# A third layer every sixteenth step: the units of a small network folded once more by DMA

## The chip, the cores and the metric

The kernel runs on one core of one Trainium2 chip. The metric is the time of one execution on the device, in microseconds (us). The kernel before was run three times; one more execution was profiled.

## What is computed

The reference chains four layers on an image of 2 x 512 channels x 32 x 32 pixels. Only the first, a deformable attention block, is touched here. Of it, one piece matters: a bias on the attention scores that a small network of three layers computes for each pair of a pixel and a sampling point.

```
pos  = grid_q[:, :, None, :] - grid_kv[:, None, :, :]
bias = jnp.sign(pos) * jnp.log1p(jnp.abs(pos))
bias = jax.nn.relu(bias @ cpb_w1 + cpb_b1)
bias = jax.nn.relu(bias @ cpb_w2 + cpb_b2)
bias = (bias @ cpb_w3 + cpb_b3).reshape(b, GROUPS, H * W, Hd * Wd)
sim  = jnp.einsum('bhid,bhjd->bhij', qh, kh) + bias
attn = jax.nn.softmax(sim, axis=-1)
```

There are 2 images with 8 groups of 64 points each, 1024 pixels, and 128 hidden units in both hidden layers. The second layer (128 to 128 units, for 1024 points x 1024 pixels) is by far the largest piece of work of the whole kernel.

## The kernel before

**Tiling.** A unit of the work is a period `t` (NT = 8 of them): 128 points, two groups. It is cut into NR = 32 steps, and a step has four points; the loop over `i` (L813) runs over all 256 steps. For each point `first` (L515) makes the first layer on VectorE in one custom instruction: 128 units on the partitions, 1024 pixels along the row, the sum of an x table and a y table, cut off below at zero. Its result stands in a ring of eleven tiles (L182 to L184); the points run AHEAD = 7 ahead of the step that uses them (L808).

**Second layer.** `second` (L536) multiplies on TensorE. The 128 output units are cut into four parts of 32 (BLOCK), taken in the order 1, 0, 3, 2. For one part, the four points of the step stand beside one another: each product takes 32 columns of the array and writes 32 partitions of a PSUM tile `z`, so a tile is four points x 32 units on the partitions and 1024 pixels along the row. There are three such PSUM tiles. ScalarE applies the bias and the relu (L552) into an SBUF tile `h2`. The weights of the third layer were taken into the second one beforehand as magnitudes; only their signs (`turn`, `w3sign`) are left to be applied.

**Folding the units.** Since the third layer only sums over units, with signs, units can be added before it. `joined` (L555) adds parts 0 and 1 on VectorE, and parts 2 and 3; then a DMA on POOL that accumulates (L832, 512 KB) adds the second sum to the first. What is left is one tile a step, four points x 32 units. Two steps then share a tile. For an even step a DMA on POOL adds the odd partitions to the even ones (L825, 256 KB), so that 16 units for each point stand on the even partitions. SP copies the even partitions of the odd step's tile to the odd partitions of the even step's (L827), and a DMA on POOL adds the odd step's odd partitions to that (L829).

**Third layer.** At every eighth step (`due`, L837) `third` (L562) multiplies four such tiles, eight points each, by a matrix of signs `w3`, into the score tile `sim` of the period. Four products stand beside one another, 32 columns each, for each half of the pixels. A slice of `w3` that begins at 24 - r puts the eight columns that aren't zero at the right rows. After the last one of a period `scores` (L575) adds the products of queries and keys, and a new chain of small pieces of work starts: `finish` of this period (softmax, transposes), `offsets` of the period after the next, `samples` of the next one. The loop takes one piece of that chain after the second and the fourth part of a step (L834, `next(behind, None)`). The last four steps of all go another way, in `finish_last` (L641).

**Order.** Nothing is scheduled by a planner: `in_order` (L60) holds each engine to the order in which the program issues its instructions, POOL's and SP's DMAs among them. What a queue waits for holds all that stands behind it.

**Tables.** `load_tabs` (L496) fetches the x and y tables for sixteen points (four steps) at a time, from DRAM, spread to all partitions: two quarters of eight points each. ScalarE scales them (L513). A quarter of the period's points is what one of the four column groups of `third` gets.

**Buffers.** The part-0 tiles, which live on as the joined ones, come from `h2p` (6 tiles, even steps) and `h2j` (3 tiles, odd steps), parts 2 from `h2b` (3), parts 1 and 3 from `h2q` (3). `simb` and `at` of the softmax come from a pool of two.

Of the kernel before, what the change touches and what calls it, by code (L numbers as in the profile page):

```python
# [19 lines left out]
P = 128  # L20
# [12 lines left out]
RCH = 8  # L33
# [47 lines left out]
def kernel(ctx: ExitStack, tc: tile.TileContext, a: dict, out: bass.AP):  # L81
# [56 lines left out]
    def layer0(l0, fold_d, t2_b, o2_b):  # L138
# [6 lines left out]
        h2j = l0.enter_context(tc.tile_pool(name="att_h2j", bufs=3))  # L145
# [79 lines left out]
        for w in (w3, w3_4):  # L225
            nc.gpsimd.memset(w, 0.0)
# [5 lines left out]
        def bias_weights():  # L232
# [3 lines left out]
            few = one.tile([P, 26], F32, name="few")  # L236
# [68 lines left out]
            nc.vector.tensor_scalar(w3[:, 24:32], w3[:, 24:32], w3sign[:, 1:2], None, ALU.mult)  # L305
            magnitude(b2h, w3_of)
# [186 lines left out]
        NCH = 2 * NR // RCH  # L493
        tabs_of = {}

        def load_tabs(c):  # L496

            t, rc = divmod(c, NCH)
            assert t in tables
            tabs_of[c] = []  # L500
            for ax in range(2):
                src = slog_d[t, ax].rearrange("(q r) i -> q r i", q=4)
                tab = two.tile([P, 2, RCH, 32], F32, name=f"tab{ax}")
                q, r = rc % 2 * 2, rc // 2 * RCH
                nc.sync.dma_start(out=tab, in_=src[q : q + 2, r : r + RCH, :].partition_broadcast(P))
                tabs_of[c].append(tab)
# [8 lines left out]
        def first(p):  # L515

            chunk, quad = divmod(p, 2 * RCH)
            quad, point = divmod(quad, RCH)
            if quad == 0 and point == 0:
                tabs_of.pop(chunk - 1, None)  # L520
                if chunk + 1 < NT * NCH:
                    load_tabs(chunk + 1)
            tx, ty = tabs_of[chunk]
            h1 = ring[p % len(ring)]

            nc.vector._custom_dve(  # L526
                TENSOR_ADD_SAT,
                out=h1.rearrange("p (y x) -> p y x", x=W),
                in0=tx[:, quad, point, :].unsqueeze(1).to_broadcast([P, H, W]),
                in1=ty[:, quad, point, :].unsqueeze(2).to_broadcast([P, H, W]),  # L530
                s0=float(np.finfo(np.float32).max),
                s1=0.0,
            )
            return h1

        def second(i, h1s, part):  # L536
# [13 lines left out]
            ring = h2q if part % 2 else h2b if part else h2j if i % 2 else h2p  # L550
# [11 lines left out]
        def third(sim, r, h2s, fours=(), halves=range(2)):  # L562

            for half in halves:
                n = slice(half * HALF, (half + 1) * HALF)
                ways = [(quad, w3[:, 24 - r : 56 - r], h2) for quad, h2 in enumerate(h2s)]
# [16 lines left out]
        def finish(t, sim):  # L583
# [4 lines left out]
            simb = two.tile([P, HW], F32, name="simb", tag="simb")  # L588
# [10 lines left out]
            at = two.tile([P, 8, P], F32, name="at", tag="simb")  # L599
# [41 lines left out]
        def finish_last(sim, eights, fours):  # L641
# [6 lines left out]
            simb = two.tile([P, HW], F32, name="simb", tag="simb")  # L648
# [7 lines left out]
            at = two.tile([P, 8, P], F32, name="at", tag="simb")  # L656
# [156 lines left out]
        for i in range(steps):  # L813
            for k, part in enumerate((1, 0, 3, 2)):
# [8 lines left out]
                if i < steps - 2:  # L823
                    if i >= 2 and i % 2 == 0 and k == 0:
                        nc.gpsimd.dma_start(out=joins[i - 2][0:P:2], in_=joins[i - 2][1:P:2], accum_op=ALU.add)  # L825
                    if i >= 3 and i % 2 and k == 0:
                        nc.sync.dma_start(out=joins[i - 3][1:P:2], in_=joins[i - 2][0:P:2])  # L827
                    if i >= 3 and i % 2 and k == 3:
                        nc.gpsimd.dma_start(out=joins[i - 3][1:P:2], in_=joins.pop(i - 2)[1:P:2], accum_op=ALU.add)  # L829
                if k == 1 and i - 1 in parts:  # L830
                    other = joined(parts.pop(i - 1), 2)
                    nc.gpsimd.dma_start(out=joins[i - 1], in_=other, accum_op=ALU.add)  # L832
                if k % 2:
# [4 lines left out]
                if k == 1 and due >= 0 and due % 8 == 0:  # L838
# [3 lines left out]
                    third(sim, r, [joins.pop(due + j) for j in range(0, 8, 2)])  # L842
                    if r == NR - 8:
# [1336 lines left out]
```

## Time and profile before

| | us |
|---|---|
| median of 3 runs (lowest, highest) | 3402.58 (3399.19, 3405.2) |
| the profiled execution's own time | 3400.25 |
| its span in the profile | 3398.4 |
| from the first to the last product of the second layer | 57.2 to 2001.4 |

| in that stretch of 1944.2 us | busy us |
|---|---|
| TensorE (products) | 1932.5 |
| VectorE | 1852.0 |
| ScalarE | 1412.1 |
| GpSimd (POOL) | 440.6 |
| the 16 DMA engines, mean share | 0.67 |

The profile gives for each group of equal instructions the line of the program, the engine, what is written and read, the count, then the busy time in all and the mean of one in ns, then the idle time of the engine just before them and what ended most of it. Busy time of the products is a model: they are pipelined and overlap, four of them at once where they take 32 columns each, so the time that a piece of work takes on TensorE is read better from the distance of one start to the next. A row of the timeline has the start, the time that it took, engine, line and operation, how many alike were merged into it, and in brackets the idle time before it and what ended that.

### The profile page before, as it was taken

The numbers are of one execution on the slowest core, as the hardware profiler recorded it, in microseconds if no ns is written. First come the engines' busy times: TensorE is split into PE (matmuls) and PEld (weight loads), VectorE is DVE, ScalarE is ACT, GpSimd is POOL, SyncE is SP. The second block draws the span as 40 slices with busy tenths as digits, with TensorE's granted clock in tenths as the row PEclk, the third lists the DMA queues.
The fourth block names the chain that finished last, engine by engine and source line by source line (L and its number), as shares of the span: only waits on it lengthen the run. The fifth ranks groups of instructions, "written<-read, shape, count | busy, mean of one in ns | idle before, by whom it ended". The sixth has DMA issues, their size and how long they took to land.

```text
span 3398.4 us, 61331 instructions
## 1 busy us (share of the span) xinstructions
PE 3351.9 (99%) x24853; PEld 1615.5 (48%) x24853; DVE 2662.6 (78%) x3461; ACT 1803.4 (53%) x2764; POOL 464.0 (14%) x563
## 2 busy tenths in 40 slices
PE   9999999999999999999999999999999999999998
PEld 4333332333333333333333338999953533678676
DVE  6999999999997899999998954455456465756565
ACT  4866867867866667867867641112136245212221
POOL 0222222222221122222222210000000000000000
PEclk9999999999999999999999999999999999999999
DMA  5676676676775576676776641000100010000110
GB/s 167 149 151 139 141 153 143 139 153 138 148 149 118 110 150 138 149 148 137 150 147 142 141 124 57 14 11 11 51 0 14 26 35 14 7 7 5 28 38 30
DMA packets 146707, 320.31 MB, mean 94 GB/s; under 512 B 31088, under 2 KB 76784, under 8 KB 145648
## 3 DMA queue, kind: packets, MB, share of 16 engines
q0 software_dynamic: 56880, 199.79, 30.9%
q1 hardware_dynamic: 88240, 111.80, 10.9%
q8 instruction: 198, 3.24, 0.4%
q10 hardware_dynamic: 1296, 4.72, 0.4%
q14 instruction: 93, 0.76, 0.1%
HBM read 71.46 MB, written 10.83 MB: 24 GB/s over the span
## 4 chain that ended last, share of the span: by engine, by line
PE 77%; DVE 16%; issue 4%; ACT 2%; DMA 1%; ACTq 0%; POOL 0%; DVEq 0%; SPq 0%; POOLq 0%
PE z L543 35%; DVE wa L526 6%; PE pma L136 5%; PE pw L1392 5%; PE pmb L136 4%; DVE h L557 4%; PE pmv L1392 4%; PE score L1568 3%; PE pv L1580 3%; PE pm L1392 3%; PE score L1392 3%; DVE h L526 2%; PE pmp L136 2%; PE pp L629 2%; PE ppr L1392 1%
## 5 line engine op out<-in xcount | busy, mean ns | idle before, releaser
L543 PE MATMUL z<-wa,cpb_w 128*32 128x512 f32 x11904 | 1779.1, 593 | 6.7 <-DVE simbias L490 3.4
L552 ACT ACTIVATE h<-z,b2h 128x1024 f32<-128x1024 f32 x1024 | 1134.2, 1114 | 529.6 <-PE z L543 506.2
L543 PE MATMUL z<-h,cpb_w 128*32 128x512 f32 x4480 | 986.3, 593 | 3.3 <-ACT h L552 2.2
L543 PEld LDWEIGHTS z<-wa,cpb_w 128*32 128x32 f32 x11904 | 492.9, 110 | 883.6 <-issue 804.6
L526 DVE CUSTOM_DVE_ANT_1 wa<-tab,tab 128x1024 f32<-128x1024 f32 x744 | 878.2, 1216 | 34.0 <-PE z L543 33.9
L557 DVE SCALAR_TENSOR_TENSOR h<-h,turn,h 128x1024 f32<-128x1024 f32 x512 | 653.3, 1276 | 8.8 <-ACT h L552 8.6
L543 PEld LDWEIGHTS z<-h,cpb_w 128*32 128x32 f32 x4480 | 256.2, 110 | 335.0 <-issue 291.8
L832 POOL DMA_DIRECT2D h<-h x255 | 227.9, 894 | 1055.0 <-DVE h L557 711.4
L526 DVE CUSTOM_DVE_ANT_1 h<-tab,tab 128x1024 f32<-128x1024 f32 x280 | 332.9, 1216 | 10.5 <-PE z L543 10.4
L1214 ACT COPY p<-pma 128x128 f32<-128x128 f32 x70 | 18.6, 266 | 305.6 <-PE pma L136 305.6
L1569 ACT ACTIVATE p<-score 128x512 f32<-128x512 f32 x256 | 130.0, 626 | 81.2 <-PE score L1568 80.4
L1206 DVE TENSOR_TENSOR upper<-pma,p 128x256 f32<-128x256 f32 x70 | 29.5, 421 | 163.6 <-ACT p L1214 163.5
L825 POOL DMA_DIRECT2D h<-h x126 | 110.9, 880 | 322.4 <-DMA h<-h 319.0
L829 POOL DMA_DIRECT2D h<-h x126 | 119.0, 944 | 155.2 <-DMA h<-h 148.8
L1601 DVE TENSOR_TENSOR acc<-acc,p 128x1024 f32<-128x1024 f32 x96 | 111.1, 1217 | 20.7 <-ACT p L1569 20.6
L1568 PE MATMUL score<-q,k 64*128 64x512 f32 x512 | 120.7, 604 | 1.1 <-DVE gm L1088 1.1
L1580 PE MATMUL pv<-p,vT 128*64 128x512 f32 x512 | 116.5, 598 | 0.0
L1392 PE MATMUL pw<-p,vT 128*128 128x256 f32 x384 | 91.5, 385 | 6.9 <-DVE p L1853 6.9
L513 ACT ACTIVATE tab<-tab,pc 128x512 f32<-128x512 f32 x126 | 96.2, 763 | 0.0
L1392 PE MATMUL pmv<-wa,hc 128*128 128x256 f32 x384 | 89.7, 380 | 5.2 <-DVE u L1413 5.2
L347 ACT ACTIVATE products<-qpad,pc 128x64 f32<-128x64 f32 x252 | 85.5, 407 | 0.0
L1392 PEld LDWEIGHTS pw<-p,vT 128*128 128x128 f32 x384 | 72.4, 191 | 24.2 <-DVE p L1853 8.4
(432 smaller groups left out, 3680.2 us busy)
## 6 DMA issues: line engine op xcount, KB each, us to landing
h<-h POOLq DMA_DIRECT2D x255, 512.0 KB, 5.0
h<-h POOLq DMA_DIRECT2D x252, 256.0 KB, 4.7
tab<-slog_d SPq DMA_DIRECT2D x128, 256.0 KB, 4.6
h<-h SPq DMA_DIRECT2D x126, 256.0 KB, 2.3
r<-d SPq DMA_DIRECT2D x24, 256.0 KB, 3.5
xt<-in_xt SPq DMA_DIRECT2D x8, 512.0 KB, 7.6
wa<-in_mlp_w SPq DMA_DIRECT2D x4, 1024.0 KB, 7.9
wb<-in_mlp_w SPq DMA_DIRECT2D x16, 256.0 KB, 5.6
```

What stands on the lines that cost most here:

```text
L136: nc.tensor.matmul(pm, w, m, start=(k == 0), stop=(k == len(pairs) - 1))
L526: nc.vector._custom_dve(TENSOR_ADD_SAT, out=h1.rearrange("p (y x) -> p y x", x=W), in0=tx[:, quad, point, :].unsqueeze(1).to_broadcast([P, ...
L543: nc.tensor.matmul(z[point * 32 : point * 32 + 32, n], cpb_w2[:, lo : lo + 32], h1s[point][:, n], start=True, stop=True,)
L552: nc.scalar.activation(h2, z, AF.Relu, bias=b2h[:, part : part + 1])
L557: nc.vector.scalar_tensor_tensor(h2, h2, turn[:, part // 2 : part // 2 + 1], parts.pop(part + 1), ALU.mult, ALU.add)
L829: nc.gpsimd.dma_start(out=joins[i - 3][1:P:2], in_=joins.pop(i - 2)[1:P:2], accum_op=ALU.add)
L832: nc.gpsimd.dma_start(out=joins[i - 1], in_=other, accum_op=ALU.add)
L1392: nc.tensor.matmul(out, stationary(l, k), moving(r, k), start=start and k == 0, stop=k == nk - 1, skip_group_check=not start,)
L1568: nc.tensor.matmul(sc, ks[m][r, s * P : (s + 1) * P], qs[m][r, n], start=True, stop=True)
L1569: nc.scalar.activation(p[:, part], sc, AF.Exp, scale=64 ** -0.5)
L1580: nc.tensor.matmul(pv[half][part * 64 : part * 64 + 64], vt[s % 4][:, lo : lo + 64], lps[s, half][:, part, :], start=(s == 0), stop=(s == 7),)
L1601: nc.vector.tensor_add(acc[half], acc[half], ps[s, half])
```

## The change

It folds the units once more for the first 240 steps (all but the last sixteen). `LAST` is 240.

- Each step's tile is folded from 32 units to 16 (256 KB) in a DMA of its own on POOL, issued at the first part of the step after the next. A step whose number divides by four then folds its own tile to 8 units (128 KB). The other three steps of four copy 32 partitions into that tile (128 KB, SP), and one more accumulating DMA (128 KB, POOL) adds their other 32 partitions there. So four steps share a tile, sixteen points x 8 units.
- The third layer comes every sixteenth step, with four tiles of sixteen points and a matrix `w3_16`. It is issued after the fourth part of step due + 19, where due is the first step of its sixteen; before, it was issued after the second part of step due + 11. The chain of small pieces of a period thus starts half a step later.
- Points are taken quarter by quarter: a table holds sixteen points of one quarter in one run, where it held eight of two quarters. For the last sixteen steps the old order is kept, with the old scheme of folding.
- `h2p` now holds the tiles of every fourth step, `h2j` (now 4 tiles) the others. `simb` and `at` come from a pool of one and so share one buffer; `at` of `finish_last` comes from `h2q`.
- The weights' preparation gets four small VectorE operations for the new column pattern and two for the matrix.

```diff
-        h2j = l0.enter_context(tc.tile_pool(name="att_h2j", bufs=3))
+        h2j = l0.enter_context(tc.tile_pool(name="att_h2j", bufs=4))
...
+            quarter = few[:, 26:28]
+            for k in range(2):
+                nc.vector.tensor_reduce(quarter[:, k : k + 1], ident[:, 2 + k : P : 4], AX.X, ALU.add)
+                nc.vector.scalar_tensor_tensor(eighth, quarter[:, k : k + 1], 8.0, eighth, ALU.mult, ALU.add)
+            nc.vector.tensor_scalar(w3_16[:, 16:32], row[:, 0:16], eighth, 0.0, ALU.add, ALU.is_equal)
+            nc.vector.tensor_scalar(w3_16[:, 16:32], w3_16[:, 16:32], w3sign[:, 1:2], None, ALU.mult)
...
-        NCH = 2 * NR // RCH
+        NCH = NR // 4
+        LAST = NT * NR - 16
...
-                tab = two.tile([P, 2, RCH, 32], F32, name=f"tab{ax}")
-                q, r = rc % 2 * 2, rc // 2 * RCH
-                nc.sync.dma_start(out=tab, in_=src[q : q + 2, r : r + RCH, :].partition_broadcast(P))
+                tab = two.tile([P, 16, 32], F32, name=f"tab{ax}")
+                if 4 * c < LAST:
+                    q, r = rc % 4, rc // 4 * 16
+                    nc.sync.dma_start(out=tab, in_=src[q, r : r + 16, :].partition_broadcast(P))
+                else:
+                    q, r = rc % 2 * 2, 16 + (rc - 4) // 2 * 8
...
-            ring = h2q if part % 2 else h2b if part else h2j if i % 2 else h2p
+            ring = h2q if part % 2 else h2b if part else h2j if i % (4 if i < LAST else 2) else h2p
...
-        def third(sim, r, h2s, fours=(), halves=range(2)):
+        def third(sim, r, h2s, fours=(), halves=range(2), wide=False):
...
-                ways = [(quad, w3[:, 24 - r : 56 - r], h2) for quad, h2 in enumerate(h2s)]
+                w = w3_16[:, 16 - r : 48 - r] if wide else w3[:, 24 - r : 56 - r]
+                ways = [(quad, w, h2) for quad, h2 in enumerate(h2s)]
...
-            simb = two.tile([P, HW], F32, name="simb", tag="simb")
+            simb = one.tile([P, HW], F32, name="simb", tag="simb")
...
-            at = two.tile([P, 8, P], F32, name="at", tag="simb")
+            at = one.tile([P, 8, P], F32, name="at", tag="simb")
...
-                if i < steps - 2:
-                    if i >= 2 and i % 2 == 0 and k == 0:
+                if LAST <= i - 2 and i < steps - 2:
+                    if i % 2 == 0 and k == 0:
                         nc.gpsimd.dma_start(out=joins[i - 2][0:P:2], in_=joins[i - 2][1:P:2], accum_op=ALU.add)
...
+                if 0 <= i - 2 < LAST:
+                    j = (i - 2) % 4
+                    whole, own = joins[i - 2 - j], joins[i - 2]
+                    if k == 0:
+                        nc.gpsimd.dma_start(out=own[0:P:2], in_=own[1:P:2], accum_op=ALU.add)
+                    if k == 3 and j == 0:
+                        nc.gpsimd.dma_start(out=own[0:P:4], in_=own[2:P:4], accum_op=ALU.add)
+                    if k == 3 and j:
+                        nc.sync.dma_start(out=whole[j:P:4], in_=own[0:P:4])
                 if k == 1 and i - 1 in parts:
                     other = joined(parts.pop(i - 1), 2)
                     nc.gpsimd.dma_start(out=joins[i - 1], in_=other, accum_op=ALU.add)
+                j = (i - 3) % 4
+                if k == 1 and 0 <= i - 3 < LAST and j:
+                    nc.gpsimd.dma_start(
+                        out=joins[i - 3 - j][j:P:4], in_=joins.pop(i - 3)[2:P:4], accum_op=ALU.add
+                    )
...
                 due = i - 11
-                if k == 1 and due >= 0 and due % 8 == 0:
+                if k == 1 and due == LAST:
+                    third(sim, 16, [joins.pop(due + j) for j in range(0, 8, 2)])
+                due = i - 19
+                if k == 3 and 0 <= due < LAST and due % 16 == 0:
                     t, r = divmod(due, NR)
                     if r == 0:
                         sim = ps_s.tile([P, HW], F32, name="sim")
-                    third(sim, r, [joins.pop(due + j) for j in range(0, 8, 2)])
-                    if r == NR - 8:
+                    third(sim, r, [joins.pop(due + j) for j in range(0, 16, 4)], wide=True)
+                    if r:
```

## The prediction

> **What bounds the kernel now.** I read the page first: the busy shares, the costliest groups, the DMA issues.
>
> ```profile
> PE 3351.9 (99%) x24853; PEld 1615.5 (48%) x24853; DVE 2662.6 (78%) x3461; ACT 1803.4 (53%) x2764; POOL 464.0 (14%) x563
> ...
> L543 PE MATMUL z<-wa,cpb_w 128*32 128x512 f32 x11904 | 1779.1, 593 | 6.7 <-DVE simbias L490 3.4
> ...
> L543 PE MATMUL z<-h,cpb_w 128*32 128x512 f32 x4480 | 986.3, 593 | 3.3 <-ACT h L552 2.2
> ...
> L526 DVE CUSTOM_DVE_ANT_1 wa<-tab,tab 128x1024 f32<-128x1024 f32 x744 | 878.2, 1216 | 34.0 <-PE z L543 33.9
> ...
> h<-h POOLq DMA_DIRECT2D x255, 512.0 KB, 5.0
> h<-h POOLq DMA_DIRECT2D x252, 256.0 KB, 4.7
> ...
> h<-h SPq DMA_DIRECT2D x126, 256.0 KB, 2.3
> ```
>
> The second layer's products (L543) run from 57.2 to 2001.4 us, and in all that time TensorE idles 10 us in front of them (6.7 + 3.3). VectorE's first layer (L526) waits for TensorE. So TensorE bounds this stage, and an instruction taken off it is worth its own length, if VectorE follows. The windows of three periods (32 steps each) tell how closely it must follow:
>
> ```profile
> 564.50:804.80 240.30, 239.07 (x2176) 74.52 (x2172) 232.96 (x213) 179.38 (x251) 55.82 (x65) 1.00 0.68 145
> 804.80:1045.10 240.30, 239.07 (x2176) 74.51 (x2172) 232.97 (x213) 179.39 (x251) 55.87 (x65) 1.00 0.70 144
> 1045.10:1315.90 270.80, 268.29 (x2240) 85.59 (x2236) 237.98 (x217) 179.85 (x251) 55.89 (x65) 1.00 0.60 129
> ```
>
> After the time stand PE, PEld, DVE, ACT, POOL, the clock, the DMA share. A period takes 240.3 us and VectorE works 233.0 of them: 7.3 us to spare. The granted clock is full. The third period holds four output projections and is longer for that.
>
> Then the timeline of TensorE at one third layer, and that of VectorE before and after it:
>
> ```profile
> 859.67 0.60 PE L543 MATMUL z<-h,cpb_w 128*32 128x512 f32 x3
> 860.10 1.90 PE L571 MATMUL sim<-h,w 128*32 128x512 f32 x16
> 861.81 0.59 PE L543 MATMUL z<-wa,cpb_w 128*32 128x512 f32 x1
> ```
>
> ```profile
> 841.91 2.35 DVE L526 CUSTOM_DVE_ANT_1 wa<-tab,tab 128x1024 f32<-128x1024 f32 x2
> 844.18 1.28 DVE L557 SCALAR_TENSOR_TENSOR h<-h,turn,h 128x1024 f32<-128x1024 f32 x1
> 845.38 2.35 DVE L526 CUSTOM_DVE_ANT_1 h<-tab,tab 128x1024 f32<-128x1024 f32 x2
> ...
> 850.00 1.23 DVE L526 CUSTOM_DVE_ANT_1 h<-tab,tab 128x1024 f32<-128x1024 f32 x1 [0.95 <-PE z L543]
> ```
>
> Groups of four products start every 0.43 us (859.24, 859.67, 860.10). A step is 16 groups, 6.86 us; a third layer is four groups, 860.10 to 861.81: **1.71 us**. VectorE repeats two firsts and a join every 3.47 us (841.91 to 845.38), so a step costs it 6.94 us, more than TensorE's bare 6.86. It catches up only while TensorE does something else.
>
> Last, POOL's queue, its whole traffic over two steps:
>
> ```profile
> 846.00 0.86 POOL L832 DMA_DIRECT2D h<-h  x1 [5.12 <-DMA h<-h]
> 846.54 1.19 POOL L829 DMA_DIRECT2D h<-h  x1
> 851.05 0.84 POOL L825 DMA_DIRECT2D h<-h  x1 [3.33 <-DMA h<-h]
> 853.85 0.86 POOL L832 DMA_DIRECT2D h<-h  x1 [1.95 <-DVE h L557]
> ```
>
> Behind each 512 KB sum (L832) the next fold stands in the queue until that sum has landed: 846.00 to 851.05.
>
> **What the skill says.** The Trainium skill, "TensorEngine Tiling (Array Packing)", Available Configurations: a 128x32 setting gives four independent tiles. The trace agrees: four products of 593 ns every 0.43 us. "DMA: Bandwidth & Descriptors", Issuing engines are not separate DMA queues: what SP and POOL issue shares the same 16 engines, so the new folds add to the load of the sums. The trace's one DMA share (0.68 to 0.70) is of these 16. Same page, Rules for kernel authors: an accumulating DMA must wait for the semaphore of an earlier one on the same bytes. The waits "<-DMA h<-h" above are that. "SBUF — State Buffer", SBUF: two separate sides: DMA traffic and engine accesses don't slow one another. The trace fits: VectorE's join took 1262 to 1286 ns through all 507 accumulating DMAs of POOL. So more DMAs should not lengthen VectorE's work.
>
> **The change, part by part.**
>
> *Third layers.* Before, 31 stand in the loop (L571, 496 products there, 16 each) and one in the finish. After, seven periods have two each; the last has a wide one and, in the old scheme, one at step 251: 16. So 15 x 1.71 = **25.7 us** leave TensorE. None lay under other work, since TensorE is the bound. The wide ones have the same shape (four tiles, 32 columns).
>
> *VectorE as the next limit.* Over a period TensorE will need 240.3 - 2 x 1.71 = 236.9 us, VectorE still 233.0. In 16 bare steps TensorE takes 16 x 6.86 + 1.71 = 111.5 us, VectorE 16 x 6.94 = 111.0. So on the mean it follows. Locally it is tight. From 850.00 to 944.55 VectorE has no gap, because the offsets' reductions (L353, six of about 0.9 us) come on top. I followed the margin, from the end of the last first that a step needs to that step's first product: 5.0 us at step 11 of the period, 1.5 us at steps 18 and 19 (step 18's last first is done at 905.0, its products begin at 906.5), 5.7 at step 22. The third layer at 860.10 lies inside this stretch and goes; 1.5 - 1.7 = -0.2, so TensorE will wait some 0.2 to 0.6 us at step 18. In the periods that start at 57.2 and 1045.1 the margin falls to 0.3 already, but there the stretch begins early or behind the projections and doesn't lose 1.7 in the same way. I take 0.4 us x 5 periods = 2 us; bounds 0 and 12 (1.7 in seven periods).
>
> *The folds on POOL and the DMA engines.* Before, two steps need two sums of 512 KB, two accumulating folds of 256 KB and one copy of 256 KB. After, each of the first 240 steps has its sum and its own 256 KB fold (same count), and a new 128 KB accumulate; three steps of four have a 128 KB copy on SP. So 240 more issues on POOL: 240 x 0.84 = 202 us of a queue that is busy 56 of 240 us, hidden. Engine time: POOL's queue takes 30.9% of 16 engines for 199.79 MB, or 84 engine-us per MB, so 128 KB cost 11.0 / 16 = 0.69 us of all engines; 240 of them 166 us. The copies move 25 MB in place of 33, about -26 us. That is +140 of 1944 us: the share rises from 0.67 to about 0.74. A 32-row accumulate isn't in the trace: the 256 KB one lands after 3.2 at best, less half its data time (0.69) 2.5 us alone; behind a 512 KB sum about 5. From above the median 4.7 of the larger DMA, from below the estimate of 2.3 us by the DMA page (Anatomy of one DMA: 2.0 us and the bytes by 436e3), which for 512 KB gives 3.2 where the trace has at least 4.5. I take 5.3 behind a sum.
>
> *Who waits.* In order on POOL: sum, last accumulate, own fold, each fourth step the second fold. A second fold that waits (own fold of the same step, about 5 us) holds the next own fold and the next sum, which can't start before anyhow. On SP a copy that waits for its fold holds a table load (needed three steps, 20 us, later). The qpad memset (L324, 1.5 us) moves half a step and stands behind two accumulates; ACT needs it half a step, 3.5 us, later: 0 if POOL isn't late, up to 2 us a period otherwise. The third layer waits for the accumulate of step due+15, issued at step due+18. With VectorE at its latest (sum issued 9.9 us into that step) it lands at about 9.9 + 0.9 + 4.5 = 15.3 us, and the third layer, now after the fourth part of the next step, comes at 7.8 + 7.0 = 14.8. So it may wait 0.5 us in six periods; at the other due time it has several us. I take 2 us in all; bounds 0 and 12. The ring h2j of four is reused five steps later, its last reader lands within four: 0.
>
> *Tables.* Same bytes, runs of 2 KB for 1 KB: 0, a slight relief of the engines. *Prologue.* Six small VectorE operations (0.15 to 0.23 us each, 1.2 us) before 30.7 us, where VectorE then waits 2.21 us for ACT: 0; without that cover 1.2. The memset on POOL: 0. *Buffers.* simb and at share one buffer; at is written after the transposes that read simb, as before: 0. The finish's at in h2q: 0, its tiles are long read.
>
> *Sum.* -25.7 + 2 + 2 = -21.7 us. The profiled execution took 3400.25 us (span 3398.4 and 1.85 around it); that gives 3378.5. The median shown is 2.3 higher, 3402.6; so **3381**.
>
> **Rivals.** *VectorE gives the gain back* (9%): its lag isn't made up, and each period loses 1.7 us. For it speaks the stretch without gaps; against it the 3.9 us that remain to VectorE per period. 3381 + 10 = 3391. *The folds come late for the third layers* (6%): each of the 16 waits 1.3 us more, and the last accumulate takes the place of what was removed: 3381 + 21 = 3402, no change. Against it: third layers waited 0.3 us in all for DMAs before. *Slower: POOL's loop becomes the bound* (5%). Sum, landing, fold, next sum is now serial in every step: landing + 0.5 + 0.84, with the median of 5.0 us 6.3 of the 7.5 us of a step (240.3 / 32). It decides from a mean landing of 6.2 us. The sums land within 4.5 to 9.2 already, and the engines get 10% more load; a mean of 6.5 makes each of 240 steps 7.85 us: 240 x 0.34 = 82 us, 3485. Against it: 5.0 x 0.74 / 0.67 is 5.5.
>
> **Chances.** Likeliest 77% (its own range 3375 to 3388), the rivals 9, 6 and 5%, 3% for more gain than the sum (below 3375). 0.2% is 6.8 us, about what a measurement of this kernel can tell from no change. Faster: 77 + 9 + 3 = 89%. The same 6%. Slower 5%. The range goes from 3374 (no stall and the spread of the runs, 3 us) to 3394, past the first rival; the second and third stay out.
>
> **What would show it.** L571's group at 280 products for 520; L543 idle by 10 to 15 us; the period near 237.5; VectorE's wait for L543 falling from 44 to about 20 us. The first rival shows as waits of L543 for L526; the second as waits of sim for DMA h; the third as POOL without gaps and relu's (L552) waiting for DMAs. Wrong from the start: a third layer that costs TensorE more than four groups, or sums that land above 6 us.

## The result and the profile after

The kernel after takes **3393.4 us** (median of 10 runs, 3391.5 to 3395.5), the kernel before 3402.2 (median of 10, 3397.0 to 3405.7). The ratio is 0.9975, with a 95% interval of 0.9966 to 0.9984. The change makes the kernel faster by 8.7 us; the forecast was 21.6 us, and its range (3374 to 3394) just holds the time. The profiled execution took 3392.5 us, with a span of 3390.7.

These are the lines of the page of after that answer to those shown of before: busy shares, costliest groups (busy us, mean ns, idle us in front and what ended it), DMA issues (KB each, us to landing).

```profile
PE 3337.9 (98%) x24613; PEld 1626.0 (48%) x24613; DVE 2662.3 (79%) x3467; ACT 1806.6 (53%) x2764; POOL 674.0 (20%) x804
...
L556 PE MATMUL z<-wa,cpb_w 128*32 128x512 f32 x11904 | 1779.1, 593 | 10.6 <-ACT h L565 7.0
...
L556 PE MATMUL z<-h,cpb_w 128*32 128x512 f32 x4480 | 984.9, 593 | 4.1 <-ACT h L565 2.9
...
L539 DVE CUSTOM_DVE_ANT_1 wa<-tab,tab 128x1024 f32<-128x1024 f32 x744 | 878.8, 1218 | 2.8 <-PE z L556 2.8
...
L539 DVE CUSTOM_DVE_ANT_1 h<-tab,tab 128x1024 f32<-128x1024 f32 x280 | 333.2, 1217 | 2.2 <-PE z L556 2.2
...
h<-h POOLq DMA_DIRECT2D x255, 512.0 KB, 5.5
h<-h POOLq DMA_DIRECT2D x252, 256.0 KB, 3.4
...
h<-h POOLq DMA_DIRECT2D x240, 128.0 KB, 5.4
h<-h SPq DMA_DIRECT2D x180, 128.0 KB, 3.6
```

TensorE executes 240 instructions fewer, as forecast. In front of the second layer's products it now idles 14.7 us (10.6 + 4.1) for 10.0 before, and it is ScalarE that ends most of that. VectorE's first layer hardly waits for TensorE any more: 2.8 and 2.2 us in its two groups, 5.0 for 44.5 before, where the forecast had about 20 left.

The windows of the same three periods of 32 steps (us, then busy us of PE, PEld, DVE, ACT and POOL, clock, DMA share, GB/s):

```profile
566.06:805.80 239.74, 237.50 (x2140) 76.31 (x2136) 232.53 (x212) 179.86 (x250) 83.77 (x98) 1.00 0.78 159
805.80:1044.59 238.79, 236.56 (x2140) 76.13 (x2136) 232.55 (x212) 179.84 (x250) 83.78 (x97) 1.00 0.77 158
1044.59:1313.68 269.09, 265.78 (x2204) 85.05 (x2200) 237.65 (x216) 179.96 (x251) 83.86 (x97) 1.00 0.68 140
```

A period takes 239.7 or 238.8 us; 236.9 was forecast for TensorE, and VectorE's 232.5 is almost unchanged (233.0). The clock is full in both kernels from the first product of the second layer to the last, so no part of the shortfall is the clock's.

**Where the time went.** On TensorE I added up, line by line, the time from the start of each weight load to the start of the next one, from the first product of the second layer to the last. The sums hold work and waits together, and they make up the whole loop:

| us | before | after | difference |
|---|---|---|---|
| second layer (L543, L556) | 1772.4 | 1775.2 | +2.8 |
| third layers (L571, L585) | 57.0 | 37.4 | -19.6 |
| product of the offsets (`po`, behind the convolution in `offsets`: L379, L385) | 2.8 | 10.0 | +7.2 |
| all others | 112.1 | 112.5 | +0.4 |
| loop | 1944.2 | 1935.0 | -9.2 |

A kernel below whose third layers never wait has 31.2 us in that row, so 25.8 us of products are gone and 6.2 us of waits have come. With 7.2 at the product of the offsets, 2.8 at the second layer and 0.4 of others, 16.6 of the 25.8 us are given back.

*The wait at the product of the offsets.* Three timelines of after at one such product, in period t = 2, whose first step begins at 528.2 us (start, duration, and in brackets the idle time and what ended it). First TensorE:

```profile
659.28 0.38 PE L385 MATMUL po<-pc,actbd 128*128 128x2 f32 x2
660.85 3.64 PE L556 MATMUL z<-wa,cpb_w 128*32 128x512 f32 x32 [1.19 <-ACT h L565]
```

Then ScalarE:

```profile
655.09 2.10 ACT L565 ACTIVATE h<-z,b2h 128x1024 f32<-128x1024 f32 x2
658.25 0.70 ACT L382 ACTIVATE actbd<-acc,pc 64x64 f32<-64x64 f32 x2 [1.06 <-DVE acc L359]
658.98 0.81 ACT L527 ACTIVATE tab<-tab,pc 128x512 f32<-128x512 f32 x1
659.70 2.10 ACT L565 ACTIVATE h<-z,b2h 128x1024 f32<-128x1024 f32 x2
```

And VectorE:

```profile
653.79 2.34 DVE L539 CUSTOM_DVE_ANT_1 wa<-tab,tab 128x1024 f32<-128x1024 f32 x2
656.07 1.27 DVE L570 SCALAR_TENSOR_TENSOR h<-h,turn,h 128x1024 f32<-128x1024 f32 x1
657.26 0.96 DVE L359 TENSOR_REDUCE acc<-products 128x64 f32<-128x448 f32 x1
658.15 1.20 DVE L539 CUSTOM_DVE_ANT_1 wa<-tab,tab 128x1024 f32<-128x1024 f32 x1
```

Read them from the bottom up. The last reduction of the convolution (L359) stands in VectorE's queue behind bulk work without a gap and ends at 658.2. ScalarE's gelu (L382) waits 1.06 us for it, and behind the gelu stand the table scaling and the two relus that free z. TensorE waits for those: 1.19 us. By the view of ScalarE's waits this happens in all seven periods that have a convolution:

```profile
ACT actbd L382 <- DVE acc L359: 7.8, 7, 1.3
```

In the kernel before, the same wait was 1.1 us, once. The margin of the first layer's units, which the forecast had followed (here to the weight load of the step's first product), falls about as it said: 5.0 us at step 11 of this period, 0.3 at step 17, for 2.0 before. At step 18, where the forecast let it run out, it is 1.1 again, because the wait at `po`, in step 17, has made TensorE late by then. It never runs out (the least in the run is 0.04 us, in the period with the output projections), and no wait of the second layer for a first-layer unit is in the views of after. The lag is paid at a small result, through a third engine.

*The wait of the third layers.* TensorE in after at the second third layer of the period before that (t = 1):

```profile
555.70 1.03 PE L585 MATMUL sim<-h,w 128*32 128x512 f32 x6
557.59 1.90 PE L585 MATMUL sim<-h,w 128*32 128x512 f32 x10 [0.86 <-DMA h<-h]
```

And POOL's queue ahead of it:

```profile
549.78 1.19 POOL L855 DMA_DIRECT2D h<-h  x1
551.06 0.83 POOL L858 DMA_DIRECT2D h<-h  x1
554.70 0.83 POOL L850 DMA_DIRECT2D h<-h  x1 [2.81 <-DMA h<-h]
557.16 0.85 POOL L848 DMA_DIRECT2D h<-h  x1 [1.64 <-DMA h<-h]
```

The last accumulate (L858) goes out at 551.06 and the trace has it land 6.49 us later, at 557.55; the third layer goes on at 557.59, 1.8 us late. By the rows of the single third layers, 4.8 of the 6.2 us are at the second one of a period (four of seven wait, 1.9 and 2.0 us at most) and 1.4 at the first. The view of line L858 gives what waits for it in the whole run, and from issue to landing:

```profile
  PEld sim L585: 7.9, 8
  PE sim L585: 2.3, 3
...
DMA to landing us min/median/max: 3.3/5.6/8.6
```

### The profile page after: what moved, and what is told of

Read it like the earlier page. It is cut to its first block, busy times and chain, and to the rows that moved or that the text cites. A ratio compares the mean times of both kernels' runs of the same rounds, so it can differ in the third digit from the quotient of the medians.

```text
span 3390.7 us, 61326 instructions
## 1 busy us (share of the span) xinstructions
PE 3337.9 (98%) x24613; PEld 1626.0 (48%) x24613; DVE 2662.3 (79%) x3467; ACT 1806.6 (53%) x2764; POOL 674.0 (20%) x804
## 4 chain that ended last, share of the span: by engine, by line
PE 72%; DVE 15%; issue 6%; DMA 4%; ACT 2%; POOL 1%; DVEq 0%; POOLq 0%; SPq 0%; ACTq 0%
PE z L556 30%; DVE wa L539 5%; PE pma L135 5%; PE pw L1423 5%; PE pmb L135 4%; DVE h L570 4%; DMA h<-h 4%; PE pmv L1423 4%; PE score L1599 3%; PE pv L1611 3%; PE pm L1423 3%; PE score L1423 3%; DVE h L539 2%; PE pmp L135 2%; PE pp L643 2%
## 5 line engine op out<-in xcount | busy, mean ns | idle before, releaser
L556 PE MATMUL z<-wa,cpb_w 128*32 128x512 f32 x11904 | 1779.1, 593 | 10.6 <-ACT h L565 7.0
L556 PE MATMUL z<-h,cpb_w 128*32 128x512 f32 x4480 | 984.9, 593 | 4.1 <-ACT h L565 2.9
L556 PEld LDWEIGHTS z<-wa,cpb_w 128*32 128x32 f32 x11904 | 501.6, 110 | 874.0 <-issue 772.3
L539 DVE CUSTOM_DVE_ANT_1 wa<-tab,tab 128x1024 f32<-128x1024 f32 x744 | 878.8, 1218 | 2.8 <-PE z L556 2.8
L570 DVE SCALAR_TENSOR_TENSOR h<-h,turn,h 128x1024 f32<-128x1024 f32 x512 | 654.4, 1278 | 9.0 <-ACT h L565 8.7
L556 PEld LDWEIGHTS z<-h,cpb_w 128*32 128x32 f32 x4480 | 261.3, 110 | 336.5 <-issue 289.4
L848 POOL DMA_DIRECT2D h<-h x240 | 203.8, 849 | 849.8 <-DMA h<-h 786.0
L539 DVE CUSTOM_DVE_ANT_1 h<-tab,tab 128x1024 f32<-128x1024 f32 x280 | 333.2, 1217 | 2.2 <-PE z L556 2.2
L855 POOL DMA_DIRECT2D h<-h x255 | 256.7, 1007 | 307.4 <-DVE h L570 193.6
L858 POOL DMA_DIRECT2D h<-h x180 | 218.8, 1216 | 7.5 <-DMA h<-h 4.1
```

The source lines that it names most:

```text
L539: nc.vector._custom_dve(TENSOR_ADD_SAT, out=h1.rearrange("p (y x) -> p y x", x=W), in0=tx[:, point, :].unsqueeze(1).to_broadcast([P, H, W] ...
L556: nc.tensor.matmul(z[point * 32 : point * 32 + 32, n], cpb_w2[:, lo : lo + 32], h1s[point][:, n], start=True, stop=True,)
L570: nc.vector.scalar_tensor_tensor(h2, h2, turn[:, part // 2 : part // 2 + 1], parts.pop(part + 1), ALU.mult, ALU.add)
L848: nc.gpsimd.dma_start(out=own[0:P:2], in_=own[1:P:2], accum_op=ALU.add)
L858: nc.gpsimd.dma_start(out=joins[i - 3 - j][j:P:4], in_=joins.pop(i - 3)[2:P:4], accum_op=ALU.add)
```

## The experiments

**Theory A**, formed from these views: the products removed were worth their length, and two waits took most of it back. VectorE's in-order queue runs late in the stretch of the offsets, and ScalarE waits there; and the third layers wait for the last accumulate. **Rival B**: VectorE's amount of work is the bound, and any wait taken away comes back as another. **Rival C**: the added DMA traffic slows everything, or a product is not worth its row. Each kernel was timed 5 to 16 times beside the kernel before, on the same chip; differences are of medians, and the kernel before had medians of 3402.2 to 3403.6 us.

The sums over TensorE's loop, made as in the table above, for the kernels that decide (each is described below):

| us | time | loop | second layer | third layers | po | others |
|---|---|---|---|---|---|---|
| before | 3402 to 3404 | 1944.2 | 1772.4 | 57.0 | 2.8 | 112.1 |
| after | 3393.4 | 1935.0 | 1775.2 | 37.4 | 10.0 | 112.5 |
| e1_later | 3379.8 | 1924.0 | 1773.8 | 31.2 | 6.6 | 112.5 |
| e5_lean | 3376.9 | 1919.6 | 1772.4 | 31.2 | 3.5 | 112.5 |
| e14_after_lean | 3378.5 | 1921.1 | 1770.9 | 35.1 | 2.6 | 112.5 |
| e4_half | 3386.7 | 1928.6 | 1780.6 | 31.4 | 2.8 | 113.8 |
| e9_half_lean | 3375.0 | 1917.1 | 1771.5 | 31.3 | 2.2 | 112.1 |
| e10_before_lean | 3401.3 | 1942.7 | 1771.4 | 57.0 | 2.2 | 112.1 |

**e1_later: the wide third layers one step later.**

```diff
-                due = i - 19
+                due = i - (20 if i < LAST else 19)
```

> The changed kernel with its wide third layers one step later (due + 20 in place of due + 19; the one of the last period stays). Theory A (two waits gave the gain back: third layers for their last fold, 8 us, and VectorE's lag by way of the offsets' last reduction, ScalarE's gelu and its relus, 7 us): the waits of sim for DMA fall from 8 us to under 2 us, the time falls by 6 to 8 us, to about 3386; the gelu's wait stays at 5 to 8 us. Rival B (VectorE is the bound, what is taken from one wait comes back in another): 3393, no change. Rival C (the additional DMA traffic slows the engines as a whole): 3393, too.

Measured: 3379.8 us (3378.8 to 3381.3), ratio 0.9929 [0.9916, 0.9943]: 13.6 us less than after, more than any of the three expected. The third layers' row falls to 31.2 us and no third layer waits for a DMA. But ScalarE's wait for the reductions falls as well, from 7.8 to 3.5 us, and po's row from 10.0 to 6.6: the chain behind the third layer moved by a step too. So this run changes two things, which e11 and e12 take apart.

**e2_gelu: the gelu one turn later in the chain.**

```diff
             table(AF.Gelu)
             if t:
                 yield
+                yield
```

> The changed kernel with one more pause of half a step between the offsets' last reduction and the gelu that reads it. Theory A: ScalarE's wait for acc falls from 7.8 us to under 1, the time by 5 to 7 us, to about 3387; the third layers still wait 6 to 9 us. Rival B: the time stays at 3393, and products of the second layer wait for firsts (L539) instead. Rival C: 3393.

Measured: 3392.8 us (3391.8 to 3393.8), ratio 0.9968 [0.9956, 0.998]: as after. The wait for the reductions is gone, po's row is down to 2.2 us and the third layers' by 3.1, but the second layer's is up by 7.7, to 1782.9, and the others' by 3.2. The time is rival B's: putting the meeting point later only moves the payment. Its sign is there only in part: TensorE waits for first-layer units for 1.4 us in six places, while ScalarE's relus now wait for VectorE's joins, which they don't in after:

```profile
ACT h L566 <- DVE h L571: 8.0, 8, 1.2
```

VectorE really is late, and it is not this one wait that costs.

**e3_both: e1_later and e2_gelu together.**

> Both edits together. Theory A: the two add up, 12 to 15 us less, 3379 to 3382, which is the time forecast at first. Rival B: 3390 or more, since VectorE has no more to give. Rival C: 3390 or more.

Measured: 3389.6 us (3388.3 to 3391.7), ratio 0.9959 [0.9945, 0.9973]: 9.8 us more than e1_later alone. The second layer's row is 1784.3. Theory A's two separate waits don't add up. The relus' waits for the joins grow to 11.2 us here.

**e4_half: the kernel before without 15 of its 31 third layers.** Folds, transfers and chain stay; the joined units of these fifteen never enter the scores. (The first product of a period's sum moves with them, from r = 0 to r = 8.)

```diff
-                    third(sim, r, [joins.pop(due + j) for j in range(0, 8, 2)])
+                    eight = [joins.pop(due + j) for j in range(0, 8, 2)]
+                    if r in (8, 24) or due == 240:
+                        third(sim, r, eight)
```

> The kernel before, without 15 of its 31 third layers in the loop: those of the first and the third eight steps of a period are left out (in the last period only the first), so the bias lacks half of its points; folds, DMAs and the chain of small pieces stay as before. Theory A: the third layers are worth their 25.7 us, and removing one just ahead of the offsets' reductions already takes VectorE's margin, so ScalarE waits for acc 3 to 7 us: 3380 to 3384, no wait of sim for DMA. Rival B: 3393 as in the changed kernel. Rival C, and that the half step by which the chain moved makes the gelu late: 3376 to 3378, and no wait for acc.

Measured: 3386.7 us (3385.8 to 3389.1), ratio 0.995 [0.9936, 0.9963]: 17 us, not 25.7, and outside all three expectations. There is not one new DMA here, and no third layer waits, so neither the traffic nor the folds explain this shortfall. The second layer's row is up by 8.2 us. The view of TensorE's waits of e4_half names ScalarE again, now at the weights' preparation (pk) and at z:

```profile
PE pk L136 <- ACT h L552: 9.2, 6, 1.6
PE z L543 <- ACT h L552: 6.8, 16, 0.7
```

The wait for the reductions that theory A expected is 1.1 us, as before. But ScalarE's relus wait more for VectorE (1.2 and 2.3 us in these two rows before):

```profile
ACT h L552 <- DVE h L557: 5.1, 12, 1.1
ACT h L552 <- DVE wa L526: 4.9, 6, 2.3
```

**e9_half_lean and e10_before_lean: the same with VectorE relieved, and the control.** Of the six rows of taps of the convolution, only the last is reduced from the second stage on; 30 of 36 taps are left out. That takes five reductions of some 0.9 us off VectorE in each period, all in the stretch of the offsets. e9 does it to e4_half, e10 to the kernel before.

```diff
-                    if kx == 5:
-                        n = 7 if ky else 6
+                    if kx == 5 and ky == 5:
+                        n = 6
```

> The kernel before without 15 of its 31 third layers (their joined units never enter the scores), as e4_half, and in the offsets' convolution of the stages from the second on only the last of six rows of taps reduced (30 of 36 taps left out). No transfer is changed against the kernel before. Theory A, in which the 9 us that e4_half fell short of the products' price are VectorE's lag in the offsets' stretch: 3376 to 3378 us. Rival B, in which a product left out is simply worth less than its row says: 3386 us, as e4_half. Rival C, in which the lag comes from elsewhere in the stage: 3381 to 3384 us.

> The control for the two lean kernels: the kernel before with nothing but the offsets' convolution cut in the same way (30 of 36 taps left out). Theory A, in which the kernel before has just enough margin on VectorE and TensorE alone sets its end: 3402 to 3404 us, no change. Rival B, in which VectorE's 5 us in each stage already cost the kernel before something: 3392 to 3399 us.

Measured: e9 3375.0 us (3374.1 to 3376.3), ratio 0.992 [0.9907, 0.9934]; e10 3401.3 (3397.1 to 3404.7), ratio 0.9998 [0.999, 1.0007]. Without the saving on TensorE the cut of VectorE's work is worth nothing that can be measured. With it, it is worth 11.7 us (3386.7 - 3375.0; 11.5 in the loop). Between e10 and e9 nothing differs but the fifteen third layers: 26.3 us in the medians, and 57.0 - 31.3 = 25.7 us in TensorE's row, with the second layer's row equal within 0.1. So a third layer is worth 1.71 us, and the half of rival C that doubts it falls.

**e14_after_lean and e5_lean: the same cut in after, and in e1_later.**

> The kernel after with nothing but the offsets' convolution cut as in the other lean kernels (30 of 36 taps left out from the second stage on), third layers at their own steps. If lag and wait are two losses that add up: the lag's part comes back (7 us at the convolution's product, 3 us elsewhere), the waits of 8 us stay, 3382 to 3385 us. If the lag makes the sums late and so the third layers too: most of both comes back, 3377 to 3380 us. If VectorE's work matters only once the third layers come later: 3390 us or more.

> The kernel after with the wide third layers one step later, as in e1_later, and in the offsets' convolution of the stages from the second on only the last of its six rows of taps reduced (30 of 36 taps left out, so that VectorE has some 5 us less in each stage, all of it in the stretch of the offsets). Theory A, in which what is still missing against the forecast is VectorE's lag in that stretch of the stage: 3374 to 3376 us, the margin of the first layer's units stays above 2 us and ScalarE's wait for the reductions is gone. Rival B, in which VectorE's lag costs nothing once the third layers come a step later: 3380 us, as e1_later.

Measured: e14 3378.5 us (3375.7 to 3380.7), ratio 0.9926 [0.9913, 0.994]; e5 3376.9 (3374.8 to 3378.1), ratio 0.9922 [0.9908, 0.9936]. In after, taking the lag away was worth 14.9 us. The loop gives 13.9: 7.4 at po, 4.3 at the second layer and 2.2 of the third layers' waits. So the time is that of e14's second case, but for another reason: the third layers got only a third of their waits back, and the lag itself cost more than the 10 us that I had put. At the same place as above, TensorE in e14 no longer stops:

```profile
655.62 0.38 PE L385 MATMUL po<-pc,actbd 128*128 128x2 f32 x2
656.01 4.06 PE L556 MATMUL z<-wa,cpb_w 128*32 128x512 f32 x34
```

because ScalarE's gelu in e14 follows its relus without a wait, though a table scaling stands behind it here too:

```profile
651.43 2.10 ACT L565 ACTIVATE h<-z,b2h 128x1024 f32<-128x1024 f32 x2
653.42 0.70 ACT L382 ACTIVATE actbd<-acc,pc 64x64 f32<-64x64 f32 x2
654.14 0.82 ACT L527 ACTIVATE tab<-tab,pc 128x512 f32<-128x512 f32 x1
```

That VectorE no longer lags is seen in the margin of the first layer's units: at steps 14, 17 and 18 of period t = 2 it is 3.1, 0.3 and 1.1 us in after, and 4.8, 4.6 and 4.3 in e14. The third layers still wait 35.1 - 31.2 = 3.9 us, all at the second one of a period.

e5 against e9, which has none of the new transfers, bounds the other half of rival C: 3376.9 - 3375.0 = 1.9 us in the medians and 2.5 in the loop are left to the added traffic and all else in which the two differ.

The same cut is worth 14.9 us to after and 2.9 us to e1_later (13.9 and 4.4 in the loop); e5 came out between its two expectations. So one step's shift of the third layers with their chain takes away most of what the lag costs, though VectorE's work per period is the same (232.6 us) and the margin in e1_later still falls to 0.3 us in that stretch.

**e11_first and e12_shift: the two halves of e1_later.** e11 moves only the first of a period's two third layers, e12 only the chain from the offsets on.

```diff
-                due = i - 19
+                due = i - (20 if i < LAST and i % 32 > 16 else 19)
```

```diff
                             finish(t, sim),
+                            iter([None] * 2),
```

> The kernel after with only the first of a stage's two wide third layers one step later (20th step and not 19th); the second, and the chain of softmax, offsets and weights behind it, stay where they were. If the waits for the last accumulate are each one's own: half of what e1_later took off the third layers' waits, 2 to 3 us, and the wait of ScalarE at the convolution stays: 3390 to 3391 us. If the order in which the chain meets the wide third layer decides most of the 13.6 us of e1_later: 3392 to 3393 us.

> The kernel after with the offsets' convolution one step later (two empty turns ahead of it in the chain) and both wide third layers where they were. If e1_later owed part of its gain to the chain's shift (its product of the offsets then no longer meets the scaling of a table on ScalarE): that product's wait falls from 7.2 us to some 3.5 us and the time to 3389 to 3390 us. If only the third layers' step counts: 3393 us as after.

Measured: e11 3389.4 us (3387.0 to 3393.1), ratio 0.9963 [0.995, 0.9977]; e12 3392.4 (3391.1 to 3394.5), ratio 0.9969 [0.9958, 0.9981]. In e11 the moved third layers wait no longer, but of the others one now waits 3.2 us (1.8 in after) and one 1.5 (1.9), so the row falls by 1.2 us only. In e12 po's row falls from 10.0 to 6.0, nearly as in e1_later (its product no longer falls in the step in which ScalarE scales a table), but the second layer's row rises by 5.6. Alone they bring 4.0 and 1.1 us, together with the second third layer 13.6.

**e6_pause: e1_later with the offsets four steps later.** The edit is e12's, with 8 for 2.

> The kernel after with the wide third layers one step later and the offsets' convolution of each stage begun four steps later (eight empty turns ahead of it in the chain), nothing left out. Theory A, in which VectorE's lag costs where its heavy stretch stands between two third layers: the third layer at the 20th step of the stage now falls inside the stretch and gives VectorE 1.8 us back there, 3375 to 3377 us. Rival B, in which the amount of VectorE's work and not its place decides: 3380 us, as e1_later.

Measured: 3383.6 us (3381.6 to 3386.6), ratio 0.9943 [0.993, 0.9957]: 3.8 us more than e1_later, so theory A as I had put it fails. po's row is at its bare 2.8 us, and the second layer's is up by 4.4. Whatever a third layer inside the stretch gave back, new waits took at least as much.

**e7_swap and e8_best: GpSimd's order, own fold behind the next sum.** The own fold (L848) moves from the step's first part to its second, behind the sum (L855). e8 has this and the edits of e1 and e6.

> The kernel after with one change: the issue of a step's own fold is put behind the sum of the next step in GpSimd's queue, so that the queue's order is sum, fold, sum and no sum stands behind a fold that waits for the sum before it. Theory of the order, in which GpSimd's serial loop of sum, landing, fold makes the last sums late for the third layers: the third layers' waits fall from 8 us to 3 us or less, 3388 to 3390 us, and GpSimd's sums wait for VectorE again and not for the folds. Rival, in which the distance of one step and a half between the last sum's issue and the third layer is too short by itself: waits and time as after, 3393 us.

> The three edits together: wide third layers a step later, offsets four steps later, own folds behind the next sum. If the waits are separate, the order of the folds adds nothing once the third layers come later: 3375 to 3377 us, as e6_pause. If GpSimd's loop also holds joined units long enough to delay VectorE's buffers, some 2 us less than e6_pause: 3373 to 3375 us. If the fold's later issue makes the last sums late again, 3380 us or more.

Measured: e7 3428.5 us (3423.8 to 3431.9), ratio 1.0077 [1.0063, 1.0091]; e8 3406.9 (3399.8 to 3410.3), ratio 1.0009 [1.0001, 1.0017]. Both expectations of e7 are wrong by 35 us or more. The fold now shares its time with the sum and lands after 6.0 us for 3.4, and the copy and the last accumulate behind it are late: the third layers' row is 63.1 us. The second layer's is up by 8.5, and that is about the price of five short falls of the clock (last section). In e8, with third layers a step later, none waits, but two others take their place, beside three falls of the clock: relus wait 14.0 us for joined tiles still read by folds, and the memset of qpad (L330) stands behind them in POOL's queue. ScalarE in e8:

```profile
ACT qpad L336 <- POOL qpad L330: 20.1, 6, 5.3
...
ACT h L565 <- DMA h<-h: 14.0, 9, 3.8
```

**e13_order and e15_later_order: the accumulate ahead of the sum.** The 128 KB accumulate (L858) moves ahead of the 512 KB sum in the same half step; e15 has this and e1's edit.

> The kernel after with one change of order: the accumulate of a folded quarter is issued ahead of the same half step's 512 KB sum in GpSimd's queue, and not behind it. If the queue makes the last accumulate late: its landing falls from 5.5 us to some 3.5 us, the third layers' waits fall from 8 us to 3 us or less, and the time to 3388 to 3390 us. If the joined units are late already, because VectorE lags or the own folds come late: the landing falls, the waits stay above 6 us, 3393 us.

> The kernel after with the wide third layers one step later and the accumulates ahead of the sums in GpSimd's queue; nothing is left out. If the later step has already covered the landing: 3379 to 3381 us, as e1_later. If sums that land later now hold joined units back, and VectorE's buffers with them: 3383 us or more. If earlier accumulates free buffers that ScalarE waited for: 3377 to 3378 us.

Measured: e13 3412.7 us (3405.0 to 3418.8), ratio 1.0028 [1.002, 1.0037]; e15 3395.5 (3387.6 to 3402.5), ratio 0.9976 [0.9968, 0.9983]. The landing did what was expected, and the time did the opposite. DMA issues of e13:

```profile
h<-h POOLq DMA_DIRECT2D x255, 512.0 KB, 5.7
h<-h POOLq DMA_DIRECT2D x252, 256.0 KB, 3.3
...
h<-h POOLq DMA_DIRECT2D x240, 128.0 KB, 3.6
```

POOL's waits in e13, for own folds (L848) and for sums (L860):

```profile
POOL h L848 <- DMA h<-h: 990.2, 236, 6.5
...
POOL h L860 <- DVE h L570: 111.8, 24, 44.0
```

and in after, where the sum is L855:

```profile
POOL h L848 <- DMA h<-h: 786.0, 225, 7.5
...
POOL h L855 <- DVE h L570: 193.6, 82, 45.4
```

The accumulate lands 2.1 us earlier (median of its own line 3.5 us for 5.6; the page's group of 240 holds the second folds too), but the sum goes out and lands later, and the next own fold waits for the sum. POOL then waits more often for its own transfers and less often for VectorE: it is the late one. The third layers' row rises to 54.6 us, a part of it at half clock. So the landing of the last accumulate alone was not what made the third layers wait. It points to the length of the loop sum, landing, own fold, next sum; no run shortens that loop, so this is not shown by itself. In the bare stretch of after from 506.4 to 549.8 us that loop goes round six times in 43.4 us, 7.2 us each (7.0 without 1.4 us in which a fold waits beyond the sum's landing), where TensorE's step takes 6.86. In e15 the third layers don't wait, and the second layer pays (1788.8 us) by the same two waits as in e8 (15.5 us for qpad, 6.4 for tiles still read) and by two falls of the clock.

## Why the prediction was wrong

The direction held, and so did the price of a third layer; the gain was 8.7 us and not 21.6, because the step on VectorE priced the wrong wait. Of the signs named, the 240 products and the idle time of 10 to 15 us (14.7) came; the period of 237.5 (239) and VectorE's remaining wait of 20 us (5.0) did not. By its steps:

- **Third layers, 15 x 1.71 = 25.7 us.** Right to 0.1 us: e9 against e10 has 25.7 in TensorE's row.
- **VectorE as the next limit, +2 (0 to 12).** This is the step that failed most. Its stretch was right, and its margin nearly (0.3 us left at step 17, 1.1 at step 18). Its price was not: I priced only a wait of the second layer for a first-layer unit, which never came. What came is ScalarE's wait for the last reduction in the same late queue, with relus behind it. Lifting the lag in after gave 14.9 us, 13.9 in the loop (7.4 at po, 4.3 at the second layer, 2.2 at third layers). e4_half had shown 11.7 without any new transfer. The control e10 allows that up to 1.5 us of each is the cut's own (its loop is that much shorter than the kernel before's). That leaves 12.4 of the 13.9, just over my upper bound of 12, for a term put at 2: I had counted one kind of payment.
- **Who waits, +2 (0 to 12).** Mis-sized: 6.2 us. The landings were nearly right (5.3 forecast for the accumulate behind a sum, 5.6 measured), but I had POOL late at one of the two due times only, the first, and gave the other "several us". That other one has 4.8 of the 6.2 us. About 2 us of the wait are VectorE's lag (e14), the rest stays with VectorE relieved.
- **POOL's loop.** As a rival it was to decide from a mean landing of 6.2 us; the median came to 5.5, as I had put against it, and it did not become the bound. But the criterion was too coarse: it set the loop against the mean step of 7.5 us. In bare stretches, with steps of 6.86 us, POOL falls behind, and the delay is met at the third layers; that this is where the 3.9 us of e14 come from is argued, not shown. e7 and e13, which lengthen the loop, show how near it was.
- **Folds, tables, prologue, buffers at 0.** The DMA share of the loop rose from 0.67 to 0.76 (0.74 forecast). VectorE's first layer takes 1217 to 1218 ns for 1216 and its join 1278 for 1276 in the groups' means, so with the added traffic it is slower by at most 0.2%. That agrees with the Trainium skill, "SBUF — State Buffer", SBUF: two separate sides.
- **The rivals.** The first (VectorE gives the gain back, 3391) was near the time and got 9%. It described the mechanism as TensorE waiting for L539, which would have shown in the views of after and doesn't. The evidence against it, 3.9 us that remain to VectorE per period, was a mean over the period; the chain meets VectorE where it is locally late.

The sum with the measured terms, in the loop: -25.8 + 7.2 + 2.8 + 6.2 + 0.4 = -9.2 us, beside 8.7 in the medians.

**What stays open:** why the lag costs 14.9 us in after and 2.9 in e1_later. e12 shows that 4.0 us of po's part come with the chain's place: in after a table scaling starts 0.7 us behind the gelu, in the kernel before 3.4 us behind it, and the prediction did not look at that. With the lag gone, as in e14, the place costs nothing; in e12 its gain was paid back at the second layer. e11 alone gave 4 us. The two together with the other third layer do more than their sum. I have no run that names the one meeting point. The best kernel that leaves nothing out is e1_later, 23.8 us faster than before, which is somewhat more than the gain forecast for the change as it was made.

## What to carry to other kernels

When work leaves the bounding engine, the next engine's margin for the bulk operands is only half of the check: list every small result of that engine which a third engine waits for in order, and ask what stands behind that wait. Test it cheaply by taking work off the suspected engine in both kernels: if it is worth nothing before and much after, the saving uncovered it. And compare a serial loop of transfers with the shortest step of its consumer, not with the mean.

## What the runs showed that I had not expected

- A 128 KB accumulate lands after 5.6 us behind a 512 KB sum and after 3.5 ahead of it, and the sum then after 5.7 for 5.5. A 256 KB fold issued right behind a sum lands after 6.0 for 3.4. So transfers of one queue that overlap share their landing, and the order inside a half step is worth 2 us to one and costs the other.
- Swaps of two neighbouring issues in POOL's queue, with the same bytes, moved the time by +35 us (e7) and +19 us (e13). The Trainium skill, "DMA: Bandwidth & Descriptors", Rules for kernel authors, has an accumulating DMA wait for an earlier one on the same bytes. The runs show the price of that rule where such waits form a ring: 786 us of POOL's waits in after, 990 in e13.
- A cut of five reductions of 0.9 us in a period was worth nothing before (0.9998 [0.999, 1.0007]), and 14.9 us over the kernel after.
- A pause of TensorE can cost more than its own length. In the loops of all these traces, each of the thirteen pauses of 2.4 us or more (four in e7, three in e8, two in e13 and e15, one in e2 and e3) has a stretch of 3.4 or 6.8 us beside it in which the granted clock is half; of five pauses of 2.0 to 2.3 us one has, and no shorter one. In such a stretch of 3.4 us 16 products start, where the full clock has 32. My estimate from this is 1.7 us for each 3.4: about 8.5 us of e7's 35 us and 5 of e13's 19, so not all of these is the queue's.
